# Attention times a gated feed-forward net: the second sequence's q projected in one piece, its k stacks moved behind q's writes, and the count and the added ones of the last sequence moved

## The chip, the cores and the metric

The kernel runs on one core of a Trainium2 chip. TensorE (PE) does the matmuls, VectorE (DVE), ScalarE (ACT) and GpSimd (POOL) the rest, and SyncE (SP) issues most DMAs. The metric is the time of one execution on the device in microseconds (us); lower is better.

## The reference

x has 8 sequences of 512 tokens with 256 features. Each sequence is normalised per token, goes through attention and through a gated net with weights of plus and minus one, and the product of both is added to x:

```python
xn = _layernorm(x, axis=-1)
s = _L0_attn_ref(xn, ...)            # 16 heads of 16, rotary q and k,
                                     # key at most 249 tokens back
g = _silu(_L0_ffn_ref(xn, ...))      # [xn, -xn] -> 1024 -> 1024 -> 256,
                                     # weights +-1, relu(h) * 2 between
x = x + s * g
```

The softmax is written without subtracting a maximum in the main path of the kernel, and a count of values that lie in safe bounds decides at the end whether a general path must run as well. With these inputs it does not run.

## The kernel before, in words

**One list sets the order.** All work is written as pieces: a place in time (in the author's own units, 42 for a sequence, `SEQ`), a cost and a function. `run` (L247) sorts them by place and calls them one after the other; a function may return more pieces, each with a delay, which are called once the summed costs have passed it. The order of calls is the order of the instructions on each engine; nothing is reordered later. The engines wait for each other by semaphores alone, so each engine's queue, SyncE's too, is worked off strictly in order.

**A sequence on PE.** The net of one sequence (`layer`, `last`) fills most of PE's time: 8 tiles of the first hidden layer, 8 tiles of the second, each 8 matmuls in half precision and 8 in single, then the output tiles z. Between these tiles stand the rest of the matmuls: the projections of the next sequence's q and k, this sequence's v, the six attention steps ("visits") and the output projection. `attention` (L981) puts the six steps at the places among the net's tiles that share the cost most evenly. For the first sequence it takes any place that is not in the set `inner`.

**An attention step** (`step`, L973) issues the scores of one set of blocks (12 matmuls, L854, into six PSUM banks), then the value matmuls (`po`, L936) of the step before, then six exponentials on ACT (L879) and up to nine masks on POOL (L899, L906). So the value matmuls of a step come one step after its masks.

**q and k.** For the second sequence (b == 1) `project` (L403) makes two halves, "a" and "b", with 2 matmul instructions each (L413; the profile counts 4 passes). DVE multiplies each with cosine and sine (L436, 2 instructions), POOL subtracts and adds (`rotate`, L514, 2 instructions, `m_qa<-m_qa,m_qb`), ACT casts the result (`split_hi`, L531, `qh`), DVE takes the rest (`split_lo`, L538, `m_qa`), and SyncE writes each part to DRAM twice (`to_dram`, L523, 512 KB each, `dq<-qh`, `dq<-m_qa`; four writes in all). `stack` (L541) reads them back in the layout that the scores need: for each group g of four heads two tiles of k and two of q (L547, 256 KB each). The delays `hi_after` and `lo_after` place the cast and the rest behind the rotation. The first group's stacks of k and of q have places of their own (`of_k` and `at`, L1007), the other groups' come together. The q of the later sequences is made in another way (`project_seven`) and is not touched.

**The divisor of attention** is gathered from the sums S over DRAM (`gather`, `pack`, `invert`, L1029 to L1061), also through SyncE's queue.

**The end.** The last sequence is done in two halves of 256 tokens. Its last two output tiles are finished by the "final" branch of `last` (L676 to L704): exponential, plus one, reciprocal, product. For tile 2 this is done in two parts of 128 columns, so that the first reciprocal can start sooner. `add_up` (L1143) sums the counts with a matmul, and DVE reduces and casts the sum (L1147, L1148). Every engine loads the result and branches at the end.

Of the kernel before, what the change touches and what calls it, by code (L numbers as in the profile page):

```python
# [15 lines left out]
AF = mybir.ActivationFunctionType  # L16
ALU = mybir.AluOpType
# [17 lines left out]
def tile_attention_times_gated_ffn(  # L35
# [42 lines left out]
    nc = tc.nc  # L78
    P = 128
    B, T, E = x.shape  # L80
# [153 lines left out]
    SEQ = 42.0  # L234
# [4 lines left out]
    quick, inner = set(), set()  # L239
# [163 lines left out]
    def project(b, what, part, half=None):  # L403

        st = states[b]
        col = E * "qk".index(what) + P * "ab".index(part)
        if half == 1:
            ps = st.pop(part)
        else:
            ps = st[part] = bank(f"{what}{part}_ps_{b}")  # L410
        for cols in [slice(0, T)] if half is None else [ts(half, T // 2)]:
            for c in range(EC):
                nc.tensor.matmul(  # L413
                    ps[:, cols], wqkv_sb[:, c, ds(col, P)], st["xT"][:, c, cols],
                    start=(c == 0), stop=(c == EC - 1),
                )
        if half == 0:
            return

        m = turned.tile(  # L420
            [P, 2, T], F32, tag=f"m{part}", name=f"m_{what}{part}_{b}",
            bufs=2,
        )
        st[what, part] = m

        hi_after, lo_after = (4.0, 5.1) if b else (5.0, 6.2) if what == "k" else (4.6, 5.4)
        if b == 1 and what == "q":
            hi_after = 3.3
        both_done = [
            (1.4, lambda: rotate(b, what)),  # L430
            (hi_after, lambda: split_hi(b, what)),
            (lo_after, lambda: split_lo(b, what)),
        ]

        def times(i):
            nc.vector.tensor_tensor(  # L436
                m[:, i], ps, rope_sb[:, i if part == "a" else 1 - i], ALU.mult
            )

        def both():  # L440
            times(0)
            times(1)
            if part == "b":
                return both_done

        return [(1.5 if b == 0 and what + part == "qb" else 0.0, both)]
# [103 lines left out]
    def prepare(b, plain=False):  # L550

        if b == 0 or plain:
            at = dict(stats=-40, norm=-38, x=-36, k=0, q=3, v=9.2)
            dp, dv = 1.5, 1.5
        else:

            at = dict(load=9, stats=9, down=10.5, over=12, norm=18.4, k=23.0, q=26.0, v=SEQ + 0.6)
            if b == 1:
                at.update(load=17.15, stats=14, down=16.9, over=17.2, norm=24.8, k=28.1, q=31.6)
            dp, dv = (0.01 if b == 1 else 1.5), 0.85  # L560
            at = {n: SEQ * (b - 1) + f for n, f in at.items()}
        out = [(at["stats"], 0, lambda: stats(b))]
        if "over" in at:
            out += [
                (at["load"], 0, lambda: load_xT(b)), (at["down"], 0, lambda: lay_down(b)),
                (at["over"], 0, lambda: lay_over(b)),
                (at["norm"], 0, lambda: norm_turned(b, 0)),
                (at["norm"] + 1.2, 0, lambda: norm_turned(b, 1)),
            ]
        for t in range(NT):  # L570
            if "over" not in at:
                out += [
                    (at["norm"] + t, 0, lambda t=t: norm(b, t)),
                    (at["x"] + t, 0.25, lambda t=t: turn_x(b, t, plain)),
                ]
            out.append((at["v"] + dv * t, 0.87, lambda t=t: project_v(b, t)))
        if b > 1 and not plain:
            for (what, phase), at_ in zip(
                itertools.product("kq", range(2)), (23.0, 24.7, 24.71, 26.4)
            ):  # L580
                out.append((
                    SEQ * (b - 1) + at_, 1.29 if phase else 1.72,
                    lambda w=what, i=phase: project_seven(b, w, i),
                ))
            return out
        for what in "kq":
            for n, part in enumerate("ab"):
                if b == 0 and what == "k" and not plain:

                    out += [  # L590
                        (-34.3 if n == 0 else -32.95, 0.87, lambda p=part: project(b, "k", p, 0)),
                        (at["k"] + dp * n, 0.87, lambda p=part: project(b, "k", p, 1)),
                    ]
                else:
                    out.append((
                        at[what] + dp * n, 1.75, lambda w=what, p=part: project(b, w, p),
                    ))
        return out


# [53 lines left out]
    def last(b, u, how):  # L654
        st = states[b]
        f, cols = outputs(b)[u]
        pz = bank(f"z_ps_{b}_{u}")
        if b + 1 == B:
            pz = pz[:, : T // 2]
        if how == "at once":  # L660
            for c in range(NF1):
                nc.tensor.matmul(
                    pz, w2[:, c, ts(f, P)].bitcast(F32), st["h2p"][:, c, cols],
                    start=(c == 0), stop=(c == NF1 - 1),
                )
        else:
            for p in "hl":
                for c in range(NF1):
                    nc.tensor.matmul(  # L669
                        pz, weights(w2, p, c, ts(f, P)), st["h2" + p][:, c, cols],  # L670
                        start=(c == 0 and p == "h"), stop=(c == NF1 - 1 and p == "l"),
                    )
        if cols.start == 0:
            st["gate of", f] = outs.tile([P, T], F32, tag=f"gate{f}", name=f"gate_{b}_{f}")
        gate = st["gate", u] = st["gate of", f][:, cols]
        if how == "final":  # L676
            residual(b, u)
            den = beside(b, u, "den")

            halves = [ts(k, T // 4) for k in range(2)]  # L680

            def ends():
                if u == 2:
                    for k in halves:
                        nc.scalar.activation(
                            den[:, k], pz[:, k], AF.Exp, scale=scales[:, 1:2]
                        )
                    return [(0.1, ready)]
                nc.scalar.activation(den, pz, AF.Exp, scale=scales[:, 1:2])
                nc.scalar.activation(den, den, AF.Identity, bias=1.0)  # L690
                return [(0.88, ready)]

            def ready():
                if u == 2:
                    for k in halves:
                        nc.vector.tensor_scalar(den[:, k], den[:, k], 1.0, None, ALU.add)
                        nc.vector.reciprocal(den[:, k], den[:, k])  # L697
                else:
                    nc.vector.reciprocal(den, den)
                nc.vector.scalar_tensor_tensor(  # L700
                    gate, pz, scales[:, 0:1], den, ALU.mult, ALU.mult
                )

            return [(0.0, ends)]  # L704

        def scale():
            nc.vector.tensor_scalar(gate, pz, scales[:, 0:1], None, ALU.mult)
            if how != "later":
                at = 7.5 if u == 0 else 11.0
                return [(at, lambda: residual(b, u)), (at, lambda: gate_ready(b, u))]  # L710

        return [(0.0, scale)]
# [268 lines left out]
    def attention(b, among):  # L981

        first, end = SEQ * b + (24.7 if b == 0 else 0.0), ends_at(b)
# [8 lines left out]
        for n in range(len(steps)):  # L992
            at = min(places, key=lambda at: abs(places[at] * len(steps) - whole * n))
# [5 lines left out]
        for g in range(NG):  # L999
            if g > 1:  # L1000
                at = of_k = times[used[g - 2][-1]] + (5.01 if b and g == 3 else 0.01)
            elif b == 0:
                of_k, at = 16.8, 17.1
            elif g:
                of_k = at = first + 0.01
            else:
                of_k, at = first - (9.0 if b == 1 else 9.8), first - (4.0 if b == 1 else 9.0)  # L1007
            if of_k == at:
                out.append((at, 0, lambda g=g: stack(b, g)))
            else:  # L1010
                out.append((of_k, 0, lambda g=g: stack(b, g, "k")))
                out.append((at, 0, lambda g=g: stack(b, g, "q")))
# [144 lines left out]
    def swap():  # L1157
# [5 lines left out]
        (-34.6, 0, signs), (-40.5, 0, lambda: warm(9)), (-34.7, 0, lambda: warm(0)),  # L1163
        (-31.0, 0, lambda: enough(0)),
        (-32.7, 0, lambda: first_parts(2, 3)),
        (19.2, 0, make_w2), (22.5, 0, swap), (24.4, 0, sum_weights), (SEQ * (B - 1) + 47.6, 0, add_up),
        (SEQ * (B - 1) + 44.0, 0, hint),
    ]
    for c in range(EC):
# [153 lines left out]
```

## Time and profile before

| | |
|---|---|
| median of 3 runs | 593.82 us (592.85 to 594.37) |
| the profiled execution | 591.66 us |
| its span, first to last instruction | 589.9 us |
| mean granted PE clock | 0.997 |
| busy: PE, DVE, ACT, POOL | 578.9, 367.9, 311.3, 307.1 us |
| DMA | 92.27 MB, mean 156 GB/s |

Rows of the profile give the line, the engine, the operation, the tiles written and read (buffer numbers left out), the count and the busy time; times are from the start of the span. PEld is the loading of weights into PE, which overlaps the matmuls. SPq is SyncE's queue: its rows are the issuing of DMAs, not the transfers. "Idle before" names the engine and line whose semaphore ended the wait, "issue" that none was seen. Times come from one profiled execution, which is shorter than the median of the runs.

### The profile page before, as it was taken

How to read it: one execution, taken by the hardware profiler on the slowest of the kernel's cores; microseconds unless marked ns; L12 is line 12 of the kernel's file. 1: busy time of each engine (PE TensorE's matmuls, PEld its weight loads, DVE VectorE, ACT ScalarE, POOL GpSimd, SP SyncE). 2: the span in 40 equal slices, each digit the busy share in tenths (PEclk: the TensorE clock that was granted, in tenths of full speed). 3: DMA queues.
4: the chain of work that ended last, by engine and by line, in shares of the span. 5: the costliest groups of instructions: out<-in, count | busy, mean ns of one | idle time of the engine just before them, and what ended most of it. 6: DMA issues, size and time to landing. Idle time of an engine off the chain costs nothing.

```text
span 589.9 us, 10715 instructions
## 1 busy us (share of the span) xinstructions
PE 578.9 (98%) x3860; PEld 378.0 (64%) x3860; DVE 367.9 (62%) x642; ACT 311.3 (53%) x603; POOL 307.1 (52%) x502
## 2 busy tenths in 40 slices
PE   7999999999999999999999999999999999999996
PEld 6665565665656656576666756667566675657785
DVE  6846436785377753778538784487744876427256
ACT  4747555545474455645455465554644645556422
POOL 2757623746346653557435574355752648335413
PEclk9999999999999999999999999999999999999998
DMA  9775743318442384414744066440863309441011
GB/s 279 286 241 168 295 138 120 110 71 321 151 124 94 127 286 142 146 61 185 266 161 146 3 256 214 148 142 2 314 226 111 110 12 349 144 146 54 24 42 41
DMA packets 50089, 92.27 MB, mean 156 GB/s; under 512 B 10992, under 2 KB 18672, under 8 KB 50032
## 3 DMA queue, kind: packets, MB, share of 16 engines
q1 hardware_dynamic: 47600, 89.31, 44.1%
q10 hardware_dynamic: 2432, 2.23, 1.3%
q8 instruction: 32, 0.52, 0.4%
q14 instruction: 25, 0.20, 0.1%
HBM read 53.22 MB, written 38.30 MB: 155 GB/s over the span
## 4 chain that ended last, share of the span: by engine, by line
PE 96%; DVE 2%; ACT 1%; DMA 1%; issue 0%; SPq 0%; DVEq 0%
PE h_ps L617 49%; PE po L936 11%; PE z_ps L669 9%; PE sc L854 8%; PE v_ps L393 5%; PE att_ps L1078 4%; PE q_ps L463 3%; PE k_ps L463 3%; PE ka_ps L413 1%; PE qb_ps L413 1%; PE kb_ps L413 1%; PE qa_ps L413 1%; DMA x<-in_x_dram 1%; ACT p L879 1%; DVE den L697 0%
## 5 line engine op out<-in xcount | busy, mean ns | idle before, releaser
L879 ACT ACTIVATE p<-sc 128x512 f32<-128x512 f32 (+2 forms) x288 | 150.7, 606 | 52.4 <-PE sc L854 47.9
L899 POOL TENSOR_SCALAR_AFFINE_SELECT p<-p 128x256 f32<-128x256 f32 (+1 forms) x224 | 96.7, 443 | 94.2 <-ACT p L879 76.9
L617 PE MATMUL h_ps<-h1l,w_sb 128*128 128x512 f32 (+1 forms) x576 | 142.7, 389 | 0.0
L617 PE MATMUL h_ps<-h1h,w_sb 128*128 128x512 f16 (+1 forms) x576 | 123.0, 356 | 0.4 <-DVE h2l L626 0.4
L617 PEld LDWEIGHTS <-w_sb 128*128 128x128 f16 x704 | 61.4, 98 | 84.1 <-issue 38.5
L617 PEld LDWEIGHTS h_ps<-h1l,w_sb 128*128 128x128 f32 x576 | 100.4, 188 | 22.2
L628 ACT ACTIVATE h2h<-h_ps 128x512 f16<-128x512 f32 (+1 forms) x72 | 39.5, 548 | 121.4 <-PE h_ps L617 121.4
L626 DVE SCALAR_TENSOR_TENSOR h2l<-h_ps,h2h 128x512 fp32r<-128x512 f32 (+1 forms) x72 | 45.1, 626 | 59.2 <-ACT h2h L628 59.0
L936 PE MATMUL po<-p,v_pad 128*32 128x378 f32 (+4 forms) x1152 | 71.5, 380 | 0.0
L626 DVE SCALAR_TENSOR_TENSOR h1l<-h_ps,h1h 128x512 fp32r<-128x512 f32 x64 | 43.1, 687 | 43.0 <-ACT h1h L628 43.0
L906 POOL TENSOR_SCALAR_AFFINE_SELECT p<-p 128x256 f32<-128x256 f32 x144 | 63.2, 439 | 0.3 <-POOL p L899 0.3
L854 PEld LDWEIGHTS sc<-q,k 64*128 64x128 f32 x576 | 41.8, 186 | 21.6 <-issue 15.0
L854 PE MATMUL sc<-q,k 64*128 64x378 f32 (+4 forms) x576 | 51.9, 310 | 1.2 <-issue 1.2
L617 PE MATMUL h_ps<-xl,w_sb 128*128 128x512 f32 x128 | 52.3, 489 | 0.0
L740 DVE RECIPROCAL den<-den 128x256 f32<-128x256 f32 (+1 forms) x32 | 50.9, 1624 | 0.8 <-ACT den L735 0.8
L628 ACT ACTIVATE h1h<-h_ps 128x512 f16<-128x512 f32 x64 | 37.6, 603 | 25.0 <-PE h_ps L617 25.0
L514 POOL TENSOR_TENSOR m_ka<-m_ka,m_kb 128x512 f32<-128x512 f32 x16 | 24.3, 1540 | 46.2 <-DVE m_kb L500 38.3
L936 PEld LDWEIGHTS po<-p,v_pad 128*32 128x32 f32 x1152 | 30.7, 109 | 21.2 <-issue 12.0
L1068 POOL TENSOR_TENSOR V<-V,R 128x512 f32<-128x512 f32 x16 | 20.5, 1283 | 40.5 <-DVE R L1067 37.6
L1107 POOL TENSOR_TENSOR gate<-gate,xr 128x512 f32<-128x512 f32 (+1 forms) x15 | 18.7, 1246 | 39.6 <-DMA xr<-in_x_t_dram 23.9
L617 PE MATMUL h_ps<-xh,w_sb 128*128 128x512 f16 x128 | 38.5, 383 | 0.0
L514 POOL TENSOR_TENSOR m_qa<-m_qa,m_qb 128x512 f32<-128x512 f32 x16 | 30.0, 1897 | 12.4 <-DVE m_qb L500 11.7
(146 smaller groups left out, 763.1 us busy)
## 6 DMA issues: line engine op xcount, KB each, us to landing
k<-dk SPq DMA_DIRECT2D x64, 256.0 KB
q<-dq SPq DMA_DIRECT2D x64, 256.0 KB
dk<-kh SPq DMA_DIRECT2D x16, 512.0 KB
dk<-m_ka SPq DMA_DIRECT2D x16, 512.0 KB
dq<-qh SPq DMA_DIRECT2D x16, 512.0 KB
dq<-m_qa SPq DMA_DIRECT2D x16, 512.0 KB
x<-in_x_dram SPq DMA_DIRECT2D x30, 128.0 KB
xT<-in_x_t_dram SPq DMA_DIRECT2D x7, 512.0 KB
```

The costliest lines, as they stand in the source:

```text
L463: nc.tensor.matmul(st["seven"][bank_][:, ts(half, H2)], a, b_, start=start and half == 0, stop=True, skip_group_check=True,)
L514: nc.gpsimd.tensor_tensor(m[:, i], m[:, i], n[:, i], op)
L617: nc.tensor.matmul(ph, weights(w, p, c, ts(f, P)), st[src + p][:, c, cols], start=(k == 0), stop=(k == n - 1),)
L626: nc.vector.scalar_tensor_tensor(lo, ph, 0.0, hi, ALU.max, ALU.subtract)
L628: high = lambda: nc.scalar.activation(hi, ph, AF.Relu)
L669: nc.tensor.matmul(pz, weights(w2, p, c, ts(f, P)), st["h2" + p][:, c, cols], start=(c == 0 and p == "h"), stop=(c == NF1 - 1 and p == "l"),)
L740: nc.vector.reciprocal(part, part)
L854: nc.tensor.matmul(sc[r + (4 if y else 2 * pair)][:, ds(at, n)], st["k", g, pair][row, ts(j, P)], st["q", g, pair][row, ds(j * P + first, n)],
L879: nc.scalar.activation(p, s_, AF.Exp, scale=D ** -0.5)
L899: nc.gpsimd.affine_select(out=block, in_=block, compare_op=ALU.is_ge, fill=0.0, base=0, pattern=[[0, heads], [1, P]], channel_multiplier=-1,)
L906: nc.gpsimd.affine_select(out=block, in_=block, compare_op=ALU.is_ge, fill=0.0, base=-1, pattern=[[0, heads], [-1, beyond]], channel_multi ...
L936: nc.tensor.matmul(po[32 * r : 32 * r + 32, ds(j * P + first, n)], v_columns(j, g, r), place(tiles_, r, y, off, n), start=(j == 0), stop=( ...
```

## The change

Five edits. The places of the second sequence's two q projections are added to `inner`, so that no attention step of the first sequence may stand between them; the fourth step then stands behind both. `hi_after` and `lo_after` of that q change from 3.3 and 5.1 to 4.4 and 5.5. The first k stacks of the second sequence move from 9.0 to 7.4 units ahead of that sequence. In the last sequence the count's sum moves from 47.6 to 43.0 units, and for output tile 2 the ones are added by ScalarE behind each exponential instead of by VectorE ahead of each reciprocal.

```diff
@@ project
         hi_after, lo_after = (4.0, 5.1) if b else (5.0, 6.2) if what == "k" else (4.6, 5.4)
         if b == 1 and what == "q":
-            hi_after = 3.3
+            hi_after, lo_after = 4.4, 5.5
@@ prepare
                     out.append((
                         at[what] + dp * n, 1.75, lambda w=what, p=part: project(b, w, p),
                     ))
+                    if b == 1 and what == "q":
+                        inner.add(at[what] + dp * n)
@@ last, ends()
                         nc.scalar.activation(
                             den[:, k], pz[:, k], AF.Exp, scale=scales[:, 1:2]
                         )
+                        nc.scalar.activation(den[:, k], den[:, k], AF.Identity, bias=1.0)
                     return [(0.1, ready)]
@@ last, ready()
                 if u == 2:
                     for k in halves:
-                        nc.vector.tensor_scalar(den[:, k], den[:, k], 1.0, None, ALU.add)
                         nc.vector.reciprocal(den[:, k], den[:, k])
@@ attention
-                of_k, at = first - (9.0 if b == 1 else 9.8), first - (4.0 if b == 1 else 9.0)
+                of_k, at = first - (7.4 if b == 1 else 9.8), first - (4.0 if b == 1 else 9.0)
@@ the list of pieces
-        (19.2, 0, make_w2), (22.5, 0, swap), (24.4, 0, sum_weights), (SEQ * (B - 1) + 47.6, 0, add_up),
+        (19.2, 0, make_w2), (22.5, 0, swap), (24.4, 0, sum_weights), (SEQ * (B - 1) + 43.0, 0, add_up),
```

On the engines this moves: on PE, qb's projection from behind the value matmuls of the fourth step to ahead of its scores, and the count's matmuls from behind z tile 2 to ahead of the last hidden tile; on DVE, qb's two products ahead of the first sequence's S_1, q's low part ahead of hidden tile 5's, the sum and cast of the count ahead of hidden tile 6's low part, and two additions of one out; on ACT, two additions of one in; on POOL, q's rotation ahead of the fourth step's nine masks; on SyncE, the first two k stacks of the second sequence behind q's four writes.

## The prediction

> **What bounds the kernel now.** I read the page first, then the waits of TensorE (PE), then SyncE's own waits and the timeline round the one place where PE stands still in mid-kernel, and last the timeline of the end.
>
> The page:
>
> ```profile
> span 589.9 us, 10715 instructions
> ...
> PE 578.9 (98%) x3860; PEld 378.0 (64%) x3860; DVE 367.9 (62%) x642; ACT 311.3 (53%) x603; POOL 307.1 (52%) x502
> ...
> PE 96%; DVE 2%; ACT 1%; DMA 1%; issue 0%; SPq 0%; DVEq 0%
> ```
>
> The kernel is a queue on PE: 96% of the chain that ended last is PE work. An edit can only gain by taking work or a hole out of that queue, or by shortening the end, where the chain leaves PE. Waits of PE's matmuls (us in total, times, longest):
>
> ```profile
> PE sc L854 <- issue: 1.2, 2, 1.0
> ```
>
> 1.2 us of holes in front of a score step. The timeline (start, duration; in brackets the idle time before) puts both at 76 to 78 us, in the first step of the second sequence:
>
> ```profile
> 61.52 2.54 POOL L514 TENSOR_TENSOR m_qa<-m_qa,m_qb 128x512 f32<-128x512 f32 x2 [0.62 <-DVE m_qb L436]
> ...
> 64.09 1.05 ACT L531 CAST qh<-m_qa 128x1024 fp32r<-128x1024 f32 x1 [4.22 <-POOL m_qa L514]
> ...
> 65.12 0.89 SPq L547 DMA_DIRECT2D k<-dk  x2
> ...
> 66.10 0.86 SPq L523 DMA_DIRECT2D dq<-qh  x2
> ...
> 67.51 1.57 SPq L523 DMA_DIRECT2D dq<-m_qa  x2
> ...
> 74.21 0.81 SPq L547 DMA_DIRECT2D q<-dq  x2
> ...
> 76.88 0.50 PE L854 MATMUL sc<-q,k 64*128 64x378 f32 x4 [1.05 <-issue]
> ...
> 77.55 0.79 PE L854 MATMUL sc<-q,k 64*128 64x378 f32 x8 [0.17 <-issue]
> ```
>
> The bracket says "issue", so the profile names no releaser; the order does. The first four matmuls read the first q stack, the next eight the second as well, and PE starts them 2.67 and 3.34 us after the first q stack was issued at 74.21. So I read 1.05 + 0.17 = 1.22 us as waiting for q. Back along it: SyncE could issue the stacks only when q's writes had landed, and q's writes stood behind the k stacks, which waited for k's writes:
>
> ```profile
> SPq L547 <- DMA dq<-m_qa: 4.6, 1, 4.6
> SPq L547 <- DMA dk<-m_ka: 3.7, 1, 3.7
> ```
>
> The end (after 579 us it runs on VectorE, DVE):
>
> ```profile
> 578.87 0.21 PE L1145 MATMUL total<-counts,ones 128*1 128x24 f32 x2
> ...
> 579.04 0.62 ACT L685 ACTIVATE den<-z_ps,scales 128x128 f32<-128x128 f32 x2 [1.51 <-PE z_ps L669]
> 579.12 0.17 DVE L1147 TENSOR_REDUCE found_f<-total 1x1 f32<-1x24 f32 x1 [1.13 <-PE total L1145]
> 579.32 0.14 DVE L1148 CAST whole<-found_f 1x1 int32<-1x1 f32 x1
> 579.44 0.23 DVE L696 TENSOR_SCALAR den<-den 128x128 f32<-128x128 f32 x1
> 579.70 0.95 DVE L697 RECIPROCAL den<-den 128x128 f32<-128x128 f32 x1
> ...
> 580.57 0.16 DVE L696 TENSOR_SCALAR den<-den 128x128 f32<-128x128 f32 x1
> ...
> 580.77 0.95 DVE L697 RECIPROCAL den<-den 128x128 f32<-128x128 f32 x1
> ```
>
> **Part 1: second sequence's q.** On PE one thing moves: qb's two instructions (four passes, 1.91 us at 58.79) go ahead of the fourth score step. Without the move PE runs qa 54.00 to 55.72, scores 1.01, values 2.06, qb, hidden tile 5 at 60.71. With it: qa to 55.72, qb to 57.44 (1.72, the row of a projection behind a projection; 1.91 is that of one behind a value step), scores to 58.45, values to 60.51, and tile 5 behind values (3.68 where such a row stands at 66.71) instead of behind qb (3.58). That is -0.19 + 0.10 = -0.09 us, and from tile 5 on the order is the old one.
>
> The others follow so. DVE: qb's two products (1.29) start at 57.45 instead of 60.74. POOL's rotation (2.54) starts when the first is done, 58.2, and ends by 60.8. ACT's cast of q stays behind the step's six exponentials. In the trace these restart 1.15 us after the values begin (56.66 to 57.81) and then run 2.05; from 58.45 that is 59.6 to 61.65. So qh lies at 61.65 to 62.7 instead of 64.09 to 65.14, and its 4.22 us wait is gone. SyncE: the gather of S_1 stands ahead of q's writes; S_1 is later by the move (values end 60.51, then 0.75 and 0.68 on DVE, so 62.0), and issuing the gather takes 1.08, so q's first write goes out at 63.05 instead of 66.10. DVE makes the low part right behind qh (1.22, to 63.95), now ahead of hidden tile 5's low part; that one needs ACT's high part from a PE tile ending at 64.2, so it loses nothing. The second write goes out at 64.0, and the k stacks at 65.6: 0.5 us later than now, just after k's writes are seen landed (65.1), so they no longer block q.
>
> From the first write's issue to the q stacks' issue took 66.10 to 74.21, 8.1 us, with 0.5 MB of k stacks in the same transfers. 63.05 + 8.1 = 71.15, and the stacks land 2.67 and 3.34 later: 73.8 and 74.5. PE asks at 75.84 - 0.09 = 75.75. **The 1.22 us vanish with 1.2 us to spare**; were it not so, each us that q is later than 75.75 would cost one us.
>
> A rule weighed here: the windows of the trace show 0.83 MB in 70 to 72 us, 414 GB/s while q is written. The Trainium skill, "DMA: Bandwidth & Descriptors", section "Specifications", gives about 358 GB/s as one core's share of HBM; by it an estimate for q's 2.1 MB is 5.9 us instead of 5.1, the spare would be 0.4 us, and the case below in which q is late still would deserve 0.1. The measured rate decides.
>
> What is moved past: POOL's nine masks of the fourth step now stand behind the rotation. The last exponential is there at 61.65; the masks run some 3.4 us without gaps (46.79 to 50.24 with them), from 60.8 to 64.3. PE's next value step asks for the first at 65.2. Cover 0.9 us for the last of them, more for the first; cost nothing. Free banks: the eight PSUM tiles qa, qb and six scores go round seven banks, so the last score tile takes qa's, which DVE has left at 57.05; PE writes it near 58. No cost. Later sequences keep their order and merely start earlier.
>
> **Part 2: the end.** The count's matmuls move from behind the third z tile to ahead of the last hidden tile. Their price: z tile to z tile is 576.96 to 579.01, 2.05 us, against 1.83 for two hidden tiles with nothing between (573.29, 575.13), so 0.22 us. PE is full there, so the third z tile, on which the exponentials wait, ends 0.22 later (bounds 0.14, from total's start at 578.87 to the next tile's at 579.01, and 0.22; I take 0.22, the difference of like rows). DVE loses the sum and cast (0.34) from 579.1 and does them near 575.9, ahead of hidden tile 7's low part and one reciprocal. The low part is then ready at 576.5 for a matmul after 577.8; the gate product of POOL that frees den's buffer ends at 578.3 instead of 578.0, ahead of the exponential at 579.3. Both cost nothing.
>
> Adding ones: two DVE instructions (0.23 + 0.16) go, two on ACT come. No row has a 128x128 one; 128x256 takes 0.42 (L690), the exponential 0.47 at 256 and 0.36 at 128, so 0.31; bounds 0.2 and 0.42. From the first exponential's start t: it ends t + 0.36, ones at t + 0.71, first reciprocal t + 0.75 to 1.70, second exponential and ones done by t + 1.35, second reciprocal ends t + 2.67. Today: 581.72 - 579.04 = 2.68. So -0.01 (bounds -0.12 and +0.10). The first half's ones replace sum, cast and add, which stood in the same gap; the second add's saving goes into starting later.
>
> Another rule: the Trainium skill, "ScalarE: Activation LUTs", "What ACT_TABLE_LOAD costs", has an ACTIVATE with immediate operands at 186 ns + 0.833 ns per column; estimated 293 ns for 128 columns, 399 for 256 where the trace has 416. By it the sum would be 0.02 better.
>
> Part 2 together: +0.2 us (0 to +0.3). No engine wants the count before its branch at the very end, so having it sooner earns nothing.
>
> **Sum.** -1.22 - 0.09 + 0.2 = -1.1 us. The profiled execution is 591.66 us, 1.76 above its span of 589.9; it becomes 590.55. The median of the three runs, 593.82, lies 2.16 above the profiled execution; with the same sum it becomes 592.7.
>
> **Rivals.**
> *The median waits longer for q than the profiled run.* PE's work hardly varies; a wait that ends with 2 MB written, read back and signalled can. For it: the runs spread over 1.5 us (592.85 to 594.37), all above the profiled one, and this is the one mid-kernel hole. Against it: starting and ending also vary, and nothing shows which. If up to all 2.16 stand there, the gain is 1.1 to 3.3: 592.0 to 590.5.
> *q is late still.* If a slower DMA takes the spare 1.2 us and as much again, the hole stays: 593.82 - 0.09 + 0.2 = 593.9. Against it: q's first write is 3 us earlier and the DMA is idle from 64 to 66 us today.
> *Slower: the masks come late.* POOL's rotation elsewhere takes 1897 ns apiece (L514 m_qa), 3.8 us. If it also starts only behind the step's exponentials, 61.65, the first three masks end near 66.6 and the last near 68.9; PE's value step, at 65.2, stands until it has them: up to 2.7 us. Sum -1.1 + 2.7 = +1.6, 595.4, and over 595.6 with slightly longer masks. It decides from the moment the first mask ends after 65.2. Against it: the products that release the rotation are done by 58.8, and the trace has 2.5 for both of them in this sequence.
> *It doesn't do what it says:* excluded; the order of instructions has the moves, and no others.
>
> **Numbers.** 0.3% (1.78 us) is about what a measurement of this kernel can tell from no change, so the sum alone is "same". Forecast 0.43; longer waits in the median 0.42; q still late 0.02; late masks or another new wait 0.13. Faster 0.42, same 0.45 (forecast and q still late), slower 0.13. The range runs from the end of the second case, 590.6, to 594.6, q still late plus half the runs' spread.
>
> **What would show it.** Right: no idle before the score matmuls near 75.8; q's first write at about 63, its stacks issued near 71; qh on ACT with no long wait on POOL; the last z tiles 0.2 us later against the last hidden tile, the second reciprocal ending 2.7 after the first exponential's start. Wrong: a PE hole before values near 65 (masks), one left at 75.8 (q), or a tail that moved by over 0.5.

## The result, and the profile after

The changed kernel takes 590.81 us (median of 22 runs, 590.19 to 592.45), the kernel before 592.38 in the same comparison (22 runs, 591.33 to 594.37). The ratio is 0.9972, 95% interval 0.9964 to 0.9981: 1.1 to 2.1 us faster. The profiled execution took 590.42 us with a span of 588.7, where 590.55 was forecast; before it was 591.66 and 589.9.

The page of the changed kernel: its span, and the shares of the chain that ended last by engine.

```profile
span 588.7 us, 10714 instructions
...
PE 97%; DVE 1%; ACT 1%; POOL 0%; issue 0%; DVEq 0%; POOLq 0%; ACTq 0%
```

PE's busy time did not fall (579.0 us against 578.9): what went is a hole. The waits of PE's matmuls (us in total, times, longest) are now these four, and no row of the score matmuls is left among them:

```profile
PE warm L245 <- POOL ident masks.py:199: 2.8, 1, 2.8
PE ka_ps L413 <- ACT xT L376: 0.5, 1, 0.5
PE h_ps L619 <- DVE h2l L628: 0.4, 1, 0.4
PE z_ps L671 <- ACT h2h L630: 0.4, 1, 0.4
```

The timeline of the second sequence's q (start, duration; idle time before in brackets):

```profile
55.82 1.88 PE L413 MATMUL qb_ps<-xT,wqkv_sb 128*128 128x512 f32 x4
...
58.52 2.52 POOL L514 TENSOR_TENSOR m_qa<-m_qa,m_qb 128x512 f32<-128x512 f32 x2 [1.99 <-DVE m_qb L436]
...
60.99 0.41 POOL L901 TENSOR_SCALAR_AFFINE_SELECT p<-p 128x256 f32<-128x256 f32 x1
...
61.71 1.07 ACT L531 CAST qh<-m_qa 128x1024 fp32r<-128x1024 f32 x1
...
62.80 0.86 SPq L523 DMA_DIRECT2D dq<-qh  x2
...
64.29 1.74 SPq L523 DMA_DIRECT2D dq<-m_qa  x2
...
65.38 1.49 PE L938 MATMUL po<-p,v_pad 128*32 128x378 f32 x24
...
66.14 2.36 SPq L547 DMA_DIRECT2D k<-dk  x2
...
71.43 1.12 SPq L547 DMA_DIRECT2D q<-dq  x2
...
75.97 1.07 PE L856 MATMUL sc<-q,k 64*128 64x378 f32 x12
```

qb stands ahead of the fourth score step, the cast of q has no wait on POOL (4.22 us before), q's first write goes out at 62.80 instead of 66.10, the k stacks behind both writes, and the q stacks at 71.43 instead of 74.21. The score matmuls at 75.97 have no bracket: they follow the hidden tile at once. The first mask starts at 60.99, well ahead of the value matmuls at 65.38, which have no idle time either.

The end:

```profile
573.92 0.21 PE L1147 MATMUL total<-counts,ones 128*1 128x24 f32 x2
...
577.98 0.37 ACT L687 ACTIVATE den<-z_ps,scales 128x128 f32<-128x128 f32 x1 [1.51 <-PE z_ps L671]
578.38 0.31 ACT L690 ACTIVATE den<-den 128x128 f32<-128x128 f32 x1
...
578.79 1.76 DVE L699 RECIPROCAL den<-den 128x128 f32<-128x128 f32 x2 [1.86 <-ACT den L690]
```

Executions differ in their first 14 us whatever the kernel, so I compare segments between rows that every trace has: from the start of qb of sequence 1 to the first z tile of sequence 2 ("middle"), and from there to the issue of the last output DMA on ACT's queue ("end"). What is left is the head (the start of qb) and the tail behind that last issue. An expectation that speaks of the first qa means a segment 1.72 us longer. All are from profiled executions, in us:

| kernel | qb starts | middle | end | span |
|---|---|---|---|---|
| before | 13.95 | 73.44 | 498.59 | 589.9 |
| after | 14.21 | 71.88 | 498.80 | 588.7 |
| front_only | 13.86 | 71.88 | 498.59 | 588.3 |
| end_only | 13.94 | 73.40 | 498.79 | 590.0 |
| count_back | 14.13 | 71.89 | 498.60 | 588.5 |
| k_stacks_back | 16.16 | 73.11 | 498.78 | 591.8 |
| k_stacks_back_2 | 14.03 | 75.19 | 498.81 | 591.8 |
| k_stacks_only | 14.08 | 75.44 | 498.60 | 592.1 |
| q_no_wait | 14.26 | 72.78 | 498.59 | 589.6 |
| q_written_more | 14.26 | 77.63 | 498.80 | 595.0 |
| before_look_1 | 14.38 | 73.43 | 498.61 | 590.5 |
| before_look_2 | 14.38 | 73.76 | 498.70 | 590.9 |
| hole_filled | 14.50 | 73.68 | 498.97 | 591.0 |
| head_filled | 14.52 | 74.61 | 498.79 | 591.8 |

So the span's 1.2 us is the sum of four: head +0.26, middle -1.56, end +0.21, tail -0.11. Head and tail wander by as much between executions of one kernel; the change itself is -1.56 + 0.21 = -1.35 us, inside the interval of the medians.

### The profile page after: what moved, and what is told of

It reads as the page before. It is cut to its first block, busy times and chain, and to the rows that moved or that the text cites. A ratio compares the mean times of both kernels' runs of the same rounds, so it can differ in the third digit from the quotient of the medians.

```text
span 588.7 us, 10714 instructions
## 1 busy us (share of the span) xinstructions
PE 579.0 (98%) x3860; PEld 378.4 (64%) x3860; DVE 368.6 (63%) x640; ACT 311.9 (53%) x605; POOL 307.4 (52%) x502
## 4 chain that ended last, share of the span: by engine, by line
PE 97%; DVE 1%; ACT 1%; POOL 0%; issue 0%; DVEq 0%; POOLq 0%; ACTq 0%
PE h_ps L619 50%; PE po L938 11%; PE z_ps L671 9%; PE sc L856 8%; PE v_ps L393 5%; PE att_ps L1080 4%; PE q_ps L463 3%; PE k_ps L463 3%; PE warm L245 1%; PE ka_ps L413 1%; PE kb_ps L413 1%; PE qa_ps L413 1%; PE qb_ps L413 1%; ACT p L881 1%; DVE den L699 0%; DVE den L701 0%
```

## The experiments

### The two halves of the change: front_only, end_only

front_only is the changed kernel without both edits at the end; end_only is the kernel before with these two alone.

```diff
front_only, against the changed kernel ("..." stands for parts of a line left out)
-                        nc.scalar.activation(den[:, k], den[:, k], AF.Identity, bias=1.0)
+                        nc.vector.tensor_scalar(den[:, k], den[:, k], 1.0, None, ALU.add)
-        ... (SEQ * (B - 1) + 43.0, 0, add_up),
+        ... (SEQ * (B - 1) + 47.6, 0, add_up),
```

> The changed kernel with both edits of the end undone: only the second sequence's q and k stacks are changed. Theory (the wait for q is gone, the end costs 0.2): 1.3 to 1.6 us faster than the kernel before, no hole in front of the scores near 76 us, and the end as before: second reciprocal 2.68 us after the start of the first exponential. Rival (most of the gain comes from the end): at most 0.5 us faster.

> The kernel before with only the two edits of the end: the count's sum earlier, ones added by ScalarE. Theory: 0.1 to 0.2 us slower than before in the profile (0.22 from the count's matmuls ahead of the last hidden tile, less 0.11 on the way through the two reciprocals), which the times cannot tell from no change; the hole near 76 us stays at 1 to 1.5 us. Rival (the end gains): 0.3 us or more faster.

front_only: 590.55 us (12 runs), ratio 0.997 (0.9956 to 0.9984). end_only: 592.94 us (12 runs), ratio 1.0003 (0.9988 to 1.0019). By the segments, front_only has all of the middle's gain and the old end, end_only the old middle and the longer end. The gain is the q part; the end costs 0.20 us, which the times alone could not have told.

### Which of the two edits at the end costs: count_back

The changed kernel with the count's sum at its old place; the ones stay on ACT.

```diff
-        ... (SEQ * (B - 1) + 43.0, 0, add_up),
+        ... (SEQ * (B - 1) + 47.6, 0, add_up),
```

> The changed kernel with the count's sum at its old place, the ones still added by ScalarE. Theory: the third z tile ends 0.22 us sooner against the hidden tiles, and VectorE's sum and cast lie in the 0.75 us in which it waits for ScalarE's exponential and ones, so the end is 0.1 to 0.3 us shorter than in the changed kernel. Rival (VectorE pays for sum and cast there): the first reciprocal starts 0.2 us or more later after the first exponential than the 0.81 us of the changed kernel, and nothing is won.

590.22 us (6 runs), ratio 0.9951 (0.9933 to 0.997); end 498.60, as before. From its timeline:

```profile
577.67 0.37 ACT L687 ACTIVATE den<-z_ps,scales 128x128 f32<-128x128 f32 x1 [1.51 <-PE z_ps L671]
...
578.49 1.76 DVE L699 RECIPROCAL den<-den 128x128 f32<-128x128 f32 x2 [0.38 <-ACT den L690]
```

All of the 0.2 is the count's move. The ones on ACT shorten first exponential to end of second reciprocal from 2.68 us to 2.58 (580.25 less 577.67), 0.10 rather than 0.01; but the last DMA is issued no sooner, so nothing of it arrives. count_back and front_only are the versions to keep, some 0.2 us ahead of the changed kernel by the segments; the times of these three overlap. Why the 0.10 does not reach the last DMA is not shown.

### The two halves of the q part: k_stacks_back, k_stacks_only

k_stacks_back is the changed kernel with the k stacks at their old place; k_stacks_only moves nothing but these. The place of qb's projection and the delays of q's cast and rest make up the other half together; they were not taken apart.

```diff
k_stacks_back, against the changed kernel; k_stacks_only is the reverse, on the kernel before
-                of_k, at = first - (7.4 if b == 1 else 9.8), ...
+                of_k, at = first - (9.0 if b == 1 else 9.8), ...
```

> The changed kernel with the first k stacks of the second sequence ahead of q's writes again. Theory (SyncE's queue is what held q): q's cast is still ready at 62.7 us, but its first write goes out only after the k stacks, near 66; the q stacks are issued near 73.5 to 74.2 and a hole of 0.4 to 1.2 us comes back in front of the scores near 76 us: 0.4 to 1.2 us slower than the changed kernel. Rival (the position of qb's projection alone did it): as fast as the changed kernel, no hole.

> The kernel before with only the k stacks' place changed: they now stand between the two writes of q's high part and the two of its low part; qb's projection stays behind the values. Theory: q's first write goes out at about 65.2 us, 0.9 sooner than 66.1, the q stacks 0 to 0.9 sooner than 74.2: 0 to 0.9 us faster than before, part of the hole left. Rival (the order of SyncE's queue alone is enough): no hole, 1.2 us or more faster.

k_stacks_back: 593.68 us (12 runs, 591.54 to 594.19), ratio 1.0006 (0.9991 to 1.0021). k_stacks_only: 594.03 us (12 runs, 592.35 to 596.07), ratio 1.002 (1.0005 to 1.0035). Neither half gains alone; k_stacks_back is 2.9 us above the changed kernel in the median, where 0.4 to 1.2 were expected; in the profiles it is 3.1, of which the middle makes 1.23 and the head 1.95. The timeline of k_stacks_back (its head is 2 us late, so read the distances):

```profile
66.84 0.88 SPq L547 DMA_DIRECT2D k<-dk  x2
...
67.81 0.86 SPq L523 DMA_DIRECT2D dq<-qh  x2
68.72 1.87 SPq L523 DMA_DIRECT2D dq<-m_qa  x2
...
76.09 0.80 SPq L547 DMA_DIRECT2D q<-dq  x2
...
78.69 0.50 PE L856 MATMUL sc<-q,k 64*128 64x378 f32 x4 [0.69 <-issue]
...
79.44 0.79 PE L856 MATMUL sc<-q,k 64*128 64x378 f32 x8 [0.25 <-issue]
```

q was ready as early as in the changed kernel (cast at 63.66, against 61.71 with a head 1.95 earlier), but its writes wait in SyncE's queue behind k stacks that wait 1.4 us for k's own writes. Most of the hole stays; the middle gains 0.33 of the 1.56. And k_stacks_only, where q is late as before (start, duration, idle before; then a table by windows: the window and its length, PE busy and count, PEld, DVE, ACT, POOL, granted PE clock, DMA share, GB/s):

```profile
77.29 0.50 PE L854 MATMUL sc<-q,k 64*128 64x378 f32 x4 [1.33 <-issue]
...
78.00 0.79 PE L854 MATMUL sc<-q,k 64*128 64x378 f32 x8 [0.21 <-DMA q<-dq]
...
78.72 3.81 PE L936 MATMUL po<-p,v_pad 128*32 128x378 f32 x40
```

```profile
78.00:80.00 2.00, 2.00 (x23) 1.21 (x27) 0.00 (x0) 0.94 (x2) 0.94 (x3) 0.75 0.73 257
80.00:82.00 2.00, 2.00 (x32) 1.24 (x24) 0.00 (x0) 1.08 (x2) 0.49 (x2) 0.50 0.77 281
82.00:84.00 2.00, 2.00 (x15) 1.25 (x8) 1.35 (x2) 0.43 (x1) 0.83 (x3) 0.90 0.00 0
```

The k stacks now wedge between q's two writes (65.29 and 68.21, against 66.10 and 67.51 before), so the hole grows by 0.3 us. The other 1.7 is new: behind the hole the granted clock falls to one half, and the 40 value matmuls take 3.81 us instead of 2.13.

### What the wait for q is worth: q_no_wait, q_written_more

q_no_wait is the kernel before, with the first q stacks of sequence 1 read from sequence 0's q, which lies in DRAM long before; that part of the attention so has another sequence's q. q_written_more is the changed kernel with four more writes of 512 KB, of qh into a DRAM buffer of their own, between q's two.

```diff
q_no_wait, in stack()
+                of = states[0] if (b, g, what) == (1, 0, "q") else st
-                rows = st["dram", what][...]
+                rows = of["dram", what][...]
q_written_more, in split_hi, behind to_dram
+        if b == 1 and what == "q":
+            more = dram.tile([P, 8, T], F32, tag="more", name=f"more_{b}", bufs=1)
+            for turn in range(4):
+                nc.sync.dma_start(more[:, ds(2 * turn, 2), :], hi.bitcast(F32))
```

> The kernel before, but the first q stacks of the second sequence are read from the first sequence's q in DRAM, which was written long before: the stacks no longer wait for q's writes (they still stand behind them in SyncE's queue), and the second sequence's first group is computed with the wrong q. Theory (the hole near 76 us is the wait for q): the stacks are issued near 69 us, no hole is left, 1.2 to 1.6 us faster than before. Rival (the hole has another cause: a PSUM bank, the fetch of instructions): the hole stays and the time is that of before.

> The changed kernel with four more writes of q's high part (512 KB each, 2.1 MB in all) to a place that nobody reads, between the writes of the high and of the low part. At the 414 GB/s of that stretch they take 5.1 us. Theory (q was 1.2 to 1.9 us early in the changed kernel, and each us after that costs one): the q stacks are issued 5.1 us later, near 76.5, PE has a hole of 3 to 4 us in front of the scores, and the time is 3 to 4 us longer than the changed kernel's. Rival (PE is held by something else there): less than 1 us longer.

q_no_wait: 591.25 us (12 runs), ratio 0.9971 (0.9957 to 0.9984), with q's projections, writes and k stacks all at their old places. Its stacks go out at 70.33 and its scores have no wait on them:

```profile
76.92 1.08 PE L855 MATMUL sc<-q,k 64*128 64x378 f32 x12
```

So it was the wait for q that cost, and not the places of the projections. Its middle, 72.78, gains 0.66 of the 1.56, the sum of two parts. From the last hidden tile to the first value matmul it takes 3.13 us against 4.63 before (-1.50; the changed kernel, 3.15, has -1.48). Ahead of that 0.84 is lost again in a new wait: in the fourth step of the first sequence the scores stand 0.46 us inside their group, on DVE's low part of a hidden tile, and the group takes 1.84 us instead of 1.01.

q_written_more: 596.29 us (7 runs), ratio 1.006 (1.004 to 1.0081).

```profile
76.11 0.80 SPq L551 DMA_DIRECT2D q<-dq  x2
...
78.86 1.95 PE L860 MATMUL sc<-q,k 64*128 64x378 f32 x12 [2.78 <-DMA q<-dq]
...
80.74 4.03 PE L942 MATMUL po<-p,v_pad 128*32 128x378 f32 x40
```

The q stacks leave 4.7 us later than in the changed kernel. 1.8 us of that is hidden, for the scores start 2.84 later (with qb 0.05 later); the rest is paid, and then paid nearly again: the middle grows by 5.75 us, because the scores take 1.95 instead of 1.07 and the values 4.03 instead of 2.13, at half the clock. So the time grew by more than the 3 to 4 us expected.

### Does the hole of the kernel before halve the clock too: hole_filled, before_look_1, before_look_2

hole_filled is the kernel before with matmuls of the identity in the hole; before_look_1 and before_look_2 are the kernel before, profiled twice more.

```diff
+        if (b, i) == (1, 0):
+            fill = bank("fill")
+            for n in range(6):
+                nc.tensor.matmul(
+                    fill[:, :P], ident, ident, start=(n == 0), stop=(n == 5)
+                )
```

> The kernel before with six matmuls of the identity put on TensorE between its last h_ps tile and the first score stack of the second sequence, so that part of the wait for q has matmuls in it; the stacks arrive as late as before. Theory (the wait costs its length and nothing else, and the spread of the runs comes from the head): the score stage still starts at about 76.9 us, the first qa of sequence 1 to the first z tile of sequence 2 stays 75.2 us, within 0.2, the median stays within 0.5 us of the kernel before (ratio 0.999 to 1.001), and single runs still differ by about 2 us according to whether the first qa starts near 12.4 or near 14.5. Rival (in runs that were not profiled the empty stretch of 1.05 us made the granted clock fall for the stages behind it, as behind the 1.33 us stretch of k_stacks_only): then filling it takes those runs away, the median falls by 0.3 to 1.0 us (ratio 0.9985 or less) and no run is more than 0.5 us above the fastest.

> The kernel before, unchanged, profiled again, to see whether its wait for q is of one length. Theory: the first qa starts near 12.4 or near 14.5 us, the empty stretches ahead of and inside the score stage of the second sequence are 1.0 and 0.2 us within 0.2 each, the granted clock stays 1.00 from 78 to 84 us, and 75.2 us pass from the first qa of sequence 1 to the first z tile of sequence 2, within 0.3. Rival: the stretches reach 1.3 us or more in some executions, the clock falls to 0.5 behind them, and the same segment is 77 us or more.

> The same kernel once more, with the same two expectations: 75.2 us within 0.3 from the first qa to the first z tile of sequence 2 by the theory, 77 us or more by the rival; the first qa near 12.4 or near 14.5 us by either.

hole_filled: 592.79 us (12 runs, 591.69 to 595.92), ratio 1.0016 (1.0001 to 1.003). The filler covers the hole, and the scores start where its end and q let them:

```profile
76.24 1.50 PE L848 MATMUL fill<-ident 128*128 128x128 f32 x12
77.67 0.50 PE L860 MATMUL sc<-q,k 64*128 64x378 f32 x4
```

The middle is 0.24 longer than before, the end 0.38 for a reason that I did not follow (the filler also takes a turn in the ring of PSUM banks, so later tiles lie in other banks), and the runs spread no less. The ratio is neither the theory's 0.999 to 1.001 nor the rival's 0.9985 or less. The two further profiles of the kernel before took 592.21 and 592.59 us; their first holes are 0.99 and 0.81 us, their clock stays 1.00, their middle 73.43 and 73.76. From the last hidden tile to the first value matmul the three profiles of the kernel before take 4.63, 4.61 and 4.39 us against 3.15 in the changed kernel, at a full clock. The rival's case, a fall of the clock behind it, is seen in none of them.

### Where the runs of one kernel differ: k_stacks_back_2, head_filled

k_stacks_back had 8 of 12 runs at 593.5 to 594.2 and 4 at 591.5 to 592.3, and its profile was of the upper kind. In it the first matmuls run at about half speed for 3 us longer than in the profile of the changed kernel (first k_stacks_back, then the changed kernel):

```profile
8.52 2.08 PE L413 MATMUL ka_ps<-xT,wqkv_sb 128*128 128x256 f32 x4 [0.46 <-ACT xT L376]
10.39 1.06 PE L368 MATMUL xnT_ps<-ident,x 128*128 128x128 f32 x4
11.24 1.63 PE L413 MATMUL kb_ps<-xT,wqkv_sb 128*128 128x256 f32 x4
```

```profile
8.47 1.16 PE L413 MATMUL ka_ps<-xT,wqkv_sb 128*128 128x256 f32 x4 [0.49 <-ACT xT L376]
9.46 0.60 PE L368 MATMUL xnT_ps<-ident,x 128*128 128x128 f32 x4
9.90 1.03 PE L413 MATMUL kb_ps<-xT,wqkv_sb 128*128 128x256 f32 x4
```

So I ran the same kernel again, and once with more matmuls in the 0.5 us ahead of ka.

```diff
head_filled, in turn_x()
+        if (b, t) == (0, 1):
+            warm(3)
```

> The kernel of k_stacks_back once more, unchanged: 8 of its 12 runs stood 1.2 us or more above its fastest (593.5 to 594.2 against 591.5 to 592.3). Theory (the spread of the runs comes from the head, where TensorE's matmuls run at half speed until about 9 us in some executions and until about 12 us in others): 4 or more of the runs again lie in an upper group some 2 us above the lower one; a profile with its first qa near 12.5 us belongs to the lower, one near 14.5 us to the upper. Rival (it comes from a wait for q of changing length): the first qa is near 12.5 us in either group and the difference stands at 76 to 82 us.

> k_stacks_back with three more matmuls of the identity on TensorE behind the first two turned tiles of x, in the stretch of 0.5 us in which it otherwise waits for xT ahead of the first ka. Theory (head): with that stretch filled the matmuls reach full speed by about 9 us in every execution; first qa near 12.5 us, no more than 2 of the runs over 1.2 us above the fastest, median 592.0 within 0.6, 1 us or more below k_stacks_back_2 of the same call. Rival (a wait for q of changing length): the filler changes nothing behind the head, the upper group is as large as in k_stacks_back_2 and the medians are within 0.4 us of each other.

k_stacks_back_2: 591.93 us (11 runs: ten from 591.39 to 592.12, one at 593.53), ratio 0.9992 (0.9982 to 1.0001). I expected four or more runs in the upper group: there was one, and it is the profiled one. Its head is good (qb at 14.03), and its excess stands where the rival put it:

```profile
76.98 0.50 PE L856 MATMUL sc<-q,k 64*128 64x378 f32 x4 [1.12 <-issue]
...
77.75 0.79 PE L856 MATMUL sc<-q,k 64*128 64x378 f32 x8 [0.26 <-issue]
...
78.47 3.57 PE L938 MATMUL po<-p,v_pad 128*32 128x378 f32 x40
```

So the theory that the spread is the head alone fell. The mean granted clock of each execution points the same way: of the 8 upper runs of k_stacks_back 3 have 0.995 or 0.996, as this profile has (0.996), and 5 have 0.997 or 0.998, as the profile with the late head has (0.998). The same instructions gave a middle of 73.11 us in one execution and 75.19 in another: 0.44 of the difference are longer holes (1.38 us against 0.94), most of the rest the half clock behind them. One kernel with a late head and one with a halved clock have the same span, 591.8.

head_filled: 593.54 us (12 runs), ratio 1.0021 (1.001 to 1.0031). Neither expectation came true, and it tells little of the head: qb starts at 14.52, 0.49 later than in k_stacks_back_2 but no later than in hole_filled, which has no such matmuls, and a new wait opens in the first sequence,

```profile
38.77 0.50 PE L858 MATMUL sc<-q,k 64*128 64x378 f32 x4 [0.86 <-DMA q<-dq]
```

after which the second sequence's holes are 1.04 and 0.44 us, at a clock of 1.00. Why q of the first sequence came later there I did not follow.

## Why the prediction was right, and where it was not

**The hole for q goes: right.** The order of events held, and their times nearly: q's first write 62.80 for 63.05, its second 64.29 for 64.0, the k stacks 66.14 for 65.6, the q stacks 71.43 for 71.15, with a head 0.26 later than the one they were worked out from. The scores follow without idle time, so the spare was there; q_written_more hid 1.8 us of lateness, where 1.2 were forecast. That the q stacks came within 0.02 us of the forecast, once these 0.26 are taken off, is luck: the first write went out 0.51 sooner than forecast, and from it to the q stacks passed 8.63 us instead of 8.1. What did not hold is that each us of lateness would cost one: in q_written_more 2.84 cost 5.75.

**Its size: the term of 1.22 was mis-sized.** Three pieces of the middle, before and after: qb to the last hidden tile ahead of the scores 59.69 and 59.61 (-0.08; -0.09 was forecast), from there to the first score matmul 3.24 and 2.15 (-1.09; -1.05), and from that to the first value matmul 1.39 and 1.00 (-0.39; -0.17). The third is the error. I took the idle row inside the group of twelve score matmuls for the price of the second wait. The group took 0.39 longer with that wait than without it, so the term is 1.48, and the middle -1.56 instead of -1.31. q_no_wait, which takes away the wait alone, gives 1.50 for the same stretch. Behind the scores nothing differs: value matmul to z tile is 9.12 us in both.

**The end: right.** +0.2 forecast, +0.21 measured, by the mechanism named (count_back gives it back whole). The ones were worth -0.10 and not -0.01, near the bound of -0.12, but the last DMA does not come sooner for it.

**The sum against the profiled execution: near.** -1.1 forecast; -1.35 by the segments. The profiled execution's 590.42 against 590.55 flatters the sum, for head and tail of that execution moved by +0.26 and -0.11.

**The level of the median: wrong step.** I put the sum under a median of 593.82 from three runs. With 22 runs the same kernel stands at 592.38. Of the 1.89 us between 592.7 and 590.81, 1.44 are this, the other 0.45 the size of the gain. The 2.16 us between profiled execution and median were taken for a property of the kernel; they were mostly three high draws. The measured time lies 0.21 above the lower end of the range, 590.6, and that end came from a rival, not from this sum: that the range held it is in part luck.

**The rivals.** *Masks late:* fell. The rotation took 2.52 us and began at 58.52, and the first mask started at 60.99. *q late still:* fell. *The median waits longer for q:* its range held the measured time, but its mechanism is not shown for the kernel before. For it: a hole of about this length did halve the clock in k_stacks_only and in one of two profiles of k_stacks_back, a step that I had not in mind, and q_no_wait gained about 1.7 us (0.9 to 2.5) in the median where its middle gained 0.66. Against it: three profiles of before with a full clock behind the hole, and a gain of the change that its segments explain.

How often the clock fell can be bounded by the mean granted clock of each execution. 3.4 us at one half take 1.7 of 592 us, or 0.003; the eleven profiles with a full clock in the middle have 0.997 to 1.0, the three with a half clock 0.996, 0.996 and 0.993. Of 94 executions of the kernel before, run beside the experiments, 7 have 0.996 or less, all at 593.5 us or more; of the changed kernel's 22 none has, of k_stacks_only's 12 eight and of q_written_more's 7 all. (One of 12 of front_only has 0.996 too, though its profile has no such hole, so the figure does not say where the clock fell.) The median of the 94 is 592.3 with these 7 or without them. So a fall of the clock may be part of the upper tail of the kernel before; it does not make the level. Whether executions without a profile wait somewhat longer at a full clock stays open. What holds up the 12 other executions of 593.5 us or more, at 0.997 to 1.0, stays open too, and so does what decides between the two heads. hole_filled decides nothing here: none of the 16 executions of the kernel before beside it fell to 0.996 either.

**The measured rate of the transfers** was reached again: the changed kernel moves 401 GB/s from 66 to 68 us, while q and k are under way. The Trainium skill, "DMA: Bandwidth & Descriptors", section "Specifications", has about 358 GB/s for one core; 401 here and 414 in the kernel before are above it. Whether the scores wait could not tell the two apart, since 0.4 us would have been left by that figure too.

## What to carry to other kernels

A wait on PE costs what the segment round it costs, not what its idle row shows: it can stretch the group that it stands in, and it can halve the clock of what follows. Two edits that each leave a chain of transfers blocked at another link can lose one by one and gain together, so try them as one and cost the chain, not the edit. Where a change is worth 0.2%, sum it over segments of the trace that leave out head and tail, and do not carry the distance between one profile and three runs over to the forecast.

## What the runs showed of the hardware

- The granted clock can fall to 0.5 behind a hole well under 2 us. Holes of 1.33 + 0.21 us (k_stacks_only) and 1.12 + 0.26 (k_stacks_back_2) were followed by about 3.4 us at half clock (windows of 2 us at 0.75, 0.50 and 0.90 lack 0.25, 0.50 and 0.10 of full speed: 1.0 + 2.0 + 0.4 us at one half), a hole of 2.78 (q_written_more, 0.55, 0.50, 0.50 and 0.74) by 6.8; holes of 1.05 + 0.17 (before), 0.99 + 0.21 and 0.81 + 0.17 (before_look_1 and before_look_2) and 1.04 + 0.44 (head_filled) were not. So length alone does not decide. The Trainium skill, "TensorE: Matmul & The Clock Gate", section "Part 1: The HAM clock gate", has the clock set by the activity in a free-running window of about 3.4 us, and half speed after an idle one. The 3.4 and 6.8 us agree with one and two such windows, and a window that does not start with the kernel would explain that like holes end both ways. That a whole window has to be idle is not what these runs show, for the longest of these holes is 2.78 us; there the measurement decides.
- One part of the head can take 2 us longer, with matmuls at about half speed until some 12 us instead of 9, while the clock's column reads 1.00 in both. The durations of the rows tell it, the column does not.
